# A graph layer pair on one core: the node's own term written into PSUM by ScalarE for two of four graphs, and the extra edges' rows made by products and a comparison

## Chip, core and metric

The kernel runs on one core of a Trainium2 chip. TensorE (PE) multiplies matrices into PSUM, VectorE (DVE), ScalarE (ACT) and GpSimd (POOL) compute element by element, and SyncE (SP) issues most transfers. Each engine works through its own queue in order and waits on semaphores for the others. The metric is device time in microseconds of one execution; the kernel before took 977.03 us, the median of three runs (973.62 to 977.51).

## What is computed

There are 128 graphs of 128 nodes with 64 features. Layer 0 sums, over the edges of each node, a small network of both ends; layer 1 multiplies with the weighted adjacency and a weight matrix.

```python
# layer 0, h = relu(layernorm(x)), mask = adj > 0
W1a, W1b = W1[:F], W1[F:]
diff = h[:, :, None, :] - h[:, None, :, :]
e = relu((h @ W1a)[:, :, None, :] + diff @ W1b + b1)     # (128, 128, 128, 192)
hm = einsum('bjkh,bjk->bjh', e, mask)
x = x + hm @ W2 + deg[..., None] * b2
# layer 1
h = relu(layernorm(x))
x = x + einsum('bnf,of->bno', einsum('bnm,bmf->bnf', adj, h), W)
```

The hidden layer splits into a part that depends on the node j alone (its own term) and a part that depends on the neighbour k alone. So an edge costs one addition of two rows, a relu and a sum. About 12% of the entries of adj are edges.

## The kernel before

Graphs are taken four at a time (G = 4, 32 groups). Within a graph the 128 neighbours are cut in four quarters, and each node gets six slots per quarter (D = 6). One-hot columns S3 say which neighbour sits in which slot; a product with k3 (three bf16 parts of the projected rows, stacked on 96 partitions) then fetches the neighbour's row. Edges beyond six in a quarter go another way, the extra edges: up to 128 per graph are listed, their rows fetched by S2 (neighbour) and R (node), rectified into X and given back to the nodes by RT.

The main work of a group is 24 jobs (class Job, L815), here called places t = 0 to 23 in the list ORDER (L916). A job takes a g tile, two PSUM banks of 128x512 f32. Of kind 0 are the first 128 hidden units of one graph b, a half jh of the nodes and a pair qp of quarters; of kind 1 are the other 64 units of two graphs at once. Six jobs make one run of the order: four of kind 0 (graph r, then graph r + 2, both qp), two of kind 1; it goes r = 0 with both halves, then r = 1 with both. So graphs 0 and 2 have t = 0 to 3 and 6 to 9, graphs 1 and 3 have t = 12 to 15 and 18 to 21, and kind 1 has t = 4, 5, 10, 11, 16, 17, 22, 23.

- Job.fill (L830), TensorE: for kind 0 two fetch products of 384 columns (g<-S,k) start the two banks, and four own-term products of 192 columns (g<-id,k) add the node's own row to all six slots. Kind 1 has twice as many, half as wide in units.
- Job.drain (L851): kind 0 is one VectorE reduction of absolute values (hm<-g); kind 1 is one ScalarE relu into T (T<-g), and GpSimd adds T up.

There are three g tiles (pool ps_g, bufs=3), which the projection tiles pp of pre_proj share, and two single-bank m tiles (ps_m) for all other products. Tables hang the rest of the work between the jobs: AHEAD (L890) prepares the next group, OWN (L905) fetches the extra edges' rows of this one, BEHIND (L909) finishes the one before. At t = 0 stands pre_adj (pt, adjT, maskT), at 1 edge_sum of the last group (pe0) and pre_rank (pq, qs), at 2 pre_norm and pre_hT (ph), at 4 edge_sum1, at 5 pre_count (pd), at 7 pre_proj for two graphs (pp; ScalarE takes ca, z and e from it, VectorE rest, GpSimd the third part of ca), at 8 post0 (py, ys), at 9 pre_edge_a (pv), at 10 post1 (pty, x1 and its statistics), at 12 pre_proj for the other two, at 14 and 15 edge_x (px, X), at 16 post3 (pga), at 19 post4 (po, the result), at 19 to 23 pre_edge_b, pre_place (pj, qj), pre_edge_c (prt, RT) and pre_edge_d (pgq, S2).

R(j, e) is 1 where extra edge e belongs to node j. It is made in steps: pre_edge_a (L620) counts by a product with a triangle how many extra edges lie before each node, and takes four absolute distances to the node's middle on ScalarE (et<-iov,mid); pre_edge_b (L649) applies four relus with the node's half width (et<-et,half) and one more for all (R<-et,ones).

All TensorE work keeps the order of the program text; on the other engines a scheduler decides the order when the kernel is built. The last group has a mixed order (ORDERL), the first runs with an order of its own (ORDER0).

Of the kernel before, what the change touches and what calls it, by code (L numbers as in the profile page):

```python
# [8 lines left out]
F32 = mybir.dt.float32  # L9
BF16 = mybir.dt.bfloat16  # L10
# [140 lines left out]
def kernel(  # L151
# [28 lines left out]
    def mm(*args, **kw):  # L180
        return tc.keep_in_program_order(nc.tensor.matmul(*args, **kw))  # L181
# [46 lines left out]
    with ExitStack() as main:  # L228
# [8 lines left out]
        def gtile(name):  # L237
            return ps_g.tile([P, 2, 512], F32, tag="g", name=name)

        def mtile(name):  # L240
            return ps_m.tile([P, 512], F32, tag="m", name=name)
# [49 lines left out]
        id32 = const.tile([P, QN], F32, tag="id32", name="id32")  # L291
        id3 = const.tile([P, QN], BF16, tag="id3", name="id3")
        upb = const.tile([P, P], BF16, tag="upb", name="upb")
        ioe = const.tile([P, E], F32, tag="ioe", name="ioe")

        def constants():
            vec.tensor_copy(identb, ident)
            vec.tensor_reduce(
                id32, ident.rearrange("p (q j) -> p j q", q=Q), AX.X, ALU.add
            )  # L300
            vec.tensor_copy(id3, id32)
            vec.tensor_copy(upb, upper)
            vec.tensor_scalar(ioe, iov, BIG, None, ALU.add)
    

# [67 lines left out]
        def weights_d():  # L373
            pl = mtile("pl")
            tp(pl[:, 0:P], wl1, ident)
            vec.tensor_copy(wl1t, pl[:, 0:P])
# [132 lines left out]
        def pre_count(g):  # L509
            d = groups[g]  # L510

            pd = mtile(f"pd{g}")
            for b in range(G):
                mm(
                    pd[:, b : b + 1], d["maskT"][:, b, :], negb, start=True, stop=True
                )
                mm(
                    pd[:, G + b : G + b + 1], d["ov"][:, b, :], oneb[:, 0:1], start=True, stop=True
                )
            d["dn"] = grp.tile([P, 2, G], F32, tag="dn", name=f"dn{g}")  # L520
            vec.tensor_copy(d["dn"].rearrange("j t b -> j (t b)"), pd[:, 0 : 2 * G])

            d["ns"] = grp.tile([P, G], F32, tag="ns", name=f"ns{g}")
            vec.scalar_tensor_tensor(
                d["ns"], pd[:, G : 2 * G], float(Q * D), d["dn"][:, 0], ALU.add, ALU.subtract
            )

            d["half"] = tmp.tile([P, G], F32, tag="half", name=f"half{g}")
            vec.tensor_scalar(
                d["half"], pd[:, G : 2 * G], -0.5, 0.5, ALU.mult, ALU.add  # L530
            )
            d["nb"] = tmp.tile([P, G], BF16, tag="nb", name=f"nb{g}")
            vec.tensor_copy(d["nb"], pd[:, G : 2 * G])

        def pre_proj(g, r):
# [67 lines left out]
            if r == 1:  # L603
                add_x()

        def pre_stack(g):

            d = groups[g]
            d["k3"] = grp.tile([K3, Q, 2, G, H], BF16, tag="k3", name=f"k3{g}")
            order = [(part, q) for part in range(3) for q in range(Q)]  # L610
            if g == 0:
                order = [(part, q) for qp in range(2) for part in range(3) for q in (2 * qp, 2 * qp + 1)]
            for part, q in order:
                sp.dma_start(
                    d["k3"][part * QN : (part + 1) * QN, q],
                    d["ca"][q * QN : (q + 1) * QN, part],
                )


        def pre_edge_a(g):  # L620
            d = groups[g]
            pv = mtile(f"pv{g}")
            mm(pv[:, 0:G], upb, d["nb"], start=True, stop=True)
            mm(pv[:, G : 2 * G], oneb, d["nb"], start=True, stop=True)
            vec.tensor_tensor(ovf, ovf, pv[:, G : 2 * G], ALU.max)

            mid = tmp.tile([P, G], F32, tag="mid", name=f"mid{g}")
            vec.tensor_tensor(mid, d["half"], pv[:, 0:G], ALU.subtract)
            d["et"] = tmp.tile([P, G, E], F32, tag="et", name=f"et{g}", bufs=1)
            for b in range(G):  # L630
                act.activation(d["et"][:, b, :], iov, AF.Abs, bias=mid[:, b : b + 1])

        def pre_place(g):

# [10 lines left out]
            )  # L645
            d["qj"] = tmp.tile([P, G, N], BF16, tag="qj", name=f"qj{g}", bufs=1)
            act.activation(d["qj"].rearrange("j b k -> j (b k)"), pj, AF.Copy)

        def pre_edge_b(g):  # L649

            d = groups[g]
            for b in range(G):
                act.activation(
                    d["et"][:, b, :], d["et"][:, b, :], AF.Relu, bias=d["half"][:, b : b + 1]
                )
            d["R"] = grp.tile([P, G, E], BF16, tag="R", name=f"R{g}")
            act.activation(d["R"], d["et"], AF.Relu, bias=ones[:, 0:1], scale=-1.0)

        def pre_edge_c(g):
            d = groups[g]  # L660
# [21 lines left out]
        def edge_x(g, r):  # L682
            d = groups[g]
            if r == 0:
                d["X"] = grp.tile([P, G, H], F32, tag="X", name=f"X{g}", bufs=1)
            px = mtile(f"px{g}_{r}")
            for p in range(2):
                b = 2 * p + r
                for t, one_hot in enumerate(("S2", "R")):
                    for i in range(3):  # L690
                        mm(
                            px[:, p * H : (p + 1) * H], d[one_hot][:, b, :], d["ca"][:, i, t, b],
                            start=t + i == 0, stop=t + i == 3,
                        )
            pxv = px[:, 0 : 2 * H].rearrange("e (p u) -> e p u", p=2)
            act.activation(d["X"][:, r::2, 0:C0], pxv[:, :, 0:C0], AF.Abs)
            act.activation(d["X"][:, r::2, C0:H], pxv[:, :, C0:H], AF.Relu)
# [114 lines left out]
            sp.dma_start(out[g * G : (g + 1) * G].rearrange("b n o -> n b o"), ot)  # L812


        class Job:  # L815
            def __init__(self, g, kind, b, jh, qp):
                self.g, self.kind, self.b, self.jh, self.qp = g, kind, b, jh, qp
                self.gt = gtile(f"g{g}_{kind}_{b}_{jh}_{qp}")

                if kind == 0:  # L820
                    self.parts = [(b, slice(0, C0), slice(0, P))]
                else:
                    self.parts = [
                        (2 * p + b, slice(C0, H), slice(p * C1, (p + 1) * C1)) for p in range(2)
                    ]

            def cols(self, rows, i):
                return self.gt[rows, i, 0:ND].rearrange("h (d j) -> h d j", d=D)

            def fill(self):  # L830

                d = groups[self.g]
                j0 = self.jh * JH
                for i in range(2):
                    q = 2 * self.qp + i
                    for b, us, rows in self.parts:
                        mm(
                            self.cols(rows, i), d["k3"][:, q, 0, b, us],
                            d["S3"][:, q, :, b * N + j0 : b * N + j0 + JH],
                            start=True, stop=False, skip_group_check=True,  # L840
                        )
                for w in range(2):
                    for i in range(2):
                        for b, us, rows in self.parts:
                            mm(
                                self.cols(rows, i)[:, :, w * QN : (w + 1) * QN],
                                d["k3"][:, 2 * self.jh + w, 1, b, us], bc(id3[0:K3, :], D, 1),
                                start=False, stop=w == 1, skip_group_check=True,
                            )
# [43 lines left out]
            7: (lambda g: pre_proj(g, 0),),  # L893
            9: (pre_edge_a,),
            12: (lambda g: pre_proj(g, 1), pre_stack,),
            19: (pre_edge_b,),
            20: (pre_place,),
            21: (pre_edge_c,),
            23: (pre_edge_d,),
        }  # L900
        OWN = {
            14: (lambda g: edge_x(g, 0),),
# [64 lines left out]
        for zs, es, second, third, add_x in steps:  # L967
# [6 lines left out]
        first_slots(0, 3)  # L974
        Engine.held = False
        early = {(f, 1) for f in (pre_adj, pre_norm)}
        FIRST = {
            2: pre_edge_a, 4: pre_place, 6: lambda g: weights_d(), 7: pre_edge_b, 9: pre_edge_d, 10: pre_edge_c
        }
        for g in range(NG):  # L980
            if 0 < g < NG - 1:
                load(g + 1)
            order = ORDER0 if g == 0 else ORDERL if g == NG - 1 else ORDER
            for t, args in enumerate(order):
                job = Job(g, *args)
                job.fill()
                job.drain()
                if g == 0 and t in FIRST:
                    FIRST[t](0)
                pieces(OWN, t, g)  # L990
                pieces(BEHIND, t, g - 1)
                pieces(AHEAD, t, g + 1)
        for t in range(T):
            pieces(BEHIND, t, NG - 1)
        om = one.tile([P, 1], F32, tag="om", name="om")
# [34 lines left out]
```

## Time and profile before

| | us |
|---|---|
| median of three runs | 977.03 |
| the profiled execution | 977.56 |
| its span, first to last instruction | 975.9 |
| VectorE drains hm<-g, 512 of 947 ns | 476.7 |
| TensorE fetch products g<-S,k, 2048 | 385.3 |
| TensorE own-term products g<-id,k, 4096 | 381.6 |
| ScalarE drains T<-g, 256 of 820 ns | 209.4 |
| ScalarE et<-iov,mid, 128 of 389 ns | 40.5 |
| ScalarE et<-et,half, 128 of 447 ns | 56.6 |
| ScalarE R<-et,ones, 32 of 759 ns | 24.3 |

The profile is of one execution. Busy times of different engines overlap, so they don't add up to the span. Products are pipelined and the profile models their ends, so a product's length in the table is more than it costs TensorE; that is read from the distances of starts, as the chain of waits lists them. The granted TensorE clock was 0.986 on the mean and full in the steady part.

### The profile page before, as it was taken

The page shows a single profiled execution, that of the slowest core. Times are in us where ns is not written, and L with a number is a line of the kernel's source. Part 1 is how long each engine was busy: PE and PEld are TensorE (multiplying, and loading weights), DVE is VectorE, ACT ScalarE, POOL GpSimd, SP SyncE. Part 2 cuts the span into 40 slices and gives each one's busy share as a digit, 9 for nine tenths or more (in the row PEclk, how much of TensorE's full clock was granted, in tenths as well). Part 3 has the DMA queues.
Part 4 walks back from the last instruction along what each step waited for, and adds up shares of the span by engine and source line. Part 5 has one row for each costly group of instructions (what it writes and reads, how often), then busy time and mean ns, then how long its engine had stood idle before and what let it go on. Part 6 is the DMA issues. An engine that isn't in the chain of part 4 may idle for free.

```text
span 975.9 us, 26737 instructions
## 1 busy us (share of the span) xinstructions
PE 944.8 (97%) x9994; PEld 692.0 (71%) x9994; DVE 798.1 (82%) x1882; ACT 699.7 (72%) x1732; POOL 745.2 (76%) x1128
## 2 busy tenths in 40 slices
PE   3899999999999999999999999999999999999996
PEld 2577777777777777777777777777777767777774
DVE  6688888888888888888888888888888888888863
ACT  5757877667887667787667887667887767787752
POOL 1478877778877778877778877778787778787793
PEclk9799999999999999999999999999999999999997
DMA  3645765655766655676655676655676655666520
GB/s 86 145 103 133 164 152 135 140 127 130 161 155 141 138 125 128 157 158 141 135 128 122 161 158 141 139 130 128 148 160 144 142 120 129 148 153 139 121 47 13
DMA packets 88293, 129.89 MB, mean 133 GB/s; under 512 B 47200, under 2 KB 63968, under 8 KB 88160
## 3 DMA queue, kind: packets, MB, share of 16 engines
q1 hardware_dynamic: 87584, 127.98, 57.9%
q8 instruction: 80, 1.31, 0.6%
q14 instruction: 53, 0.43, 0.2%
q10 hardware_dynamic: 576, 0.16, 0.1%
HBM read 13.01 MB, written 4.19 MB: 18 GB/s over the span
## 4 chain that ended last, share of the span: by engine, by line
PE 85%; DVE 5%; ACT 4%; DMA 2%; POOL 1%; issue 1%; SPq 1%; DVEq 0%; POOLq 0%; ACTq 0%
PE g L181 49%; PE pe L181 9%; PE pp L181 6%; PE px L181 6%; PE py L181 4%; PE pga L181 1%; PE po L181 1%; DVE u L198 1%; DVE S L198 1%; PE pt L184 1%; PE pj L181 1%; PE ph L184 1%; PE pty L184 1%; DVE hm L198 1%; DMA k<-ca 1%; PE pgq L181 1%
## 5 line engine op out<-in xcount | busy, mean ns | idle before, releaser
L198 POOL TENSOR_TENSOR T<-T 128x192 f32<-128x192 f32 (+2 forms) x768 | 526.7, 693 | 96.1 <-ACT T L198 56.2
L198 DVE TENSOR_REDUCE hm<-g 128x64 f32<-128x768 f32 x512 | 476.7, 947 | 85.1 <-PE g L181 83.2
L181 PEld LDWEIGHTS <-k 96*128 96x128 bf16 (+1 forms) x6144 | 412.2, 104 | 185.5 <-issue 60.7
L181 PE MATMUL g<-S,k 96*128 96x384 bf16 (+1 forms) x2048 | 385.3, 331 | 9.2 <-DMA k<-ca 7.7
L181 PE MATMUL g<-id,k 96*128 96x192 bf16 (+1 forms) x4096 | 381.6, 247 | 0.0
L198 ACT ACTIVATE T<-g 128x768 f32<-128x768 f32 x256 | 209.4, 820 | 75.1 <-PE g L181 74.1
L198 POOL TENSOR_TENSOR ca<-rest,ca 128x384 bf16<-128x384 f32 x126 | 112.6, 914 | 106.5 <-ACT ca L198 101.4
L198 ACT ACTIVATE ca<-pp 128x768 bf16<-128x768 f32 x64 | 51.4, 803 | 61.6 <-PE pp L181 59.8
L198 DVE TENSOR_TENSOR rest<-pp,ca 128x768 f32<-128x768 f32 x64 | 60.8, 950 | 16.1 <-ACT e L198 12.7
L198 ACT ACTIVATE ca<-rest 128x768 bf16<-128x768 f32 x64 | 55.1, 862 | 22.8 <-DVE rest L198 22.8
L198 DVE TENSOR_SCALAR S<-qs 128x512 bf16<-128x512 bf16 x186 | 70.5, 431 | 0.0
L181 PE MATMUL pe<-RT,X 128*64 128x128 f32 (+1 forms) x512 | 70.5, 280 | 0.0
L181 PE MATMUL pp<-wp,hT 64*128 64x448 f32 x256 | 67.8, 608 | 0.0
L198 ACT ACTIVATE z<-pp,ns 128x128 f32<-128x128 f32 (+1 forms) x256 | 65.9, 347 | 0.0
L198 ACT ACTIVATE et<-et,half 128x128 f32<-128x128 f32 x128 | 56.6, 447 | 0.0
L181 PEld LDWEIGHTS pe<-RT,X 128*64 128x64 f32 (+1 forms) x512 | 52.6, 165 | 5.3 <-issue 5.3
L198 ACT ACTIVATE qs<-pq 128x512 bf16<-128x512 f32 x32 | 19.1, 596 | 51.7 <-PE pq L181 51.7
L181 PE MATMUL px<-ca,S 128*128 128x192 bf16 x384 | 52.7, 246 | 0.0
L181 PE MATMUL px<-ca,R 128*128 128x192 bf16 x384 | 52.6, 246 | 0.0
L198 ACT ACTIVATE h<-x,mrb,rsb 128x64 f32<-128x64 f32 x128 | 51.5, 477 | 0.8 <-DVE mrb L198 0.8
L181 PE MATMUL pe<-ident,z 128*128 128x128 f32 x192 | 49.5, 285 | 0.0
L198 ACT ACTIVATE h<-x,mra,rsa 128x64 f32<-128x64 f32 x128 | 48.6, 432 | 1.1 <-DVE mra L198 1.1
(127 smaller groups left out, 1203.9 us busy)
## 6 DMA issues: line engine op xcount, KB each, us to landing
S<-S SPq DMA_DIRECT2D x372, 192.0 KB, 4.1
k<-ca SPq DMA_DIRECT2D x384, 96.0 KB, 2.2
adj<-in_adj_dram SPq DMA_DIRECT2D x32, 256.0 KB, 2.9
x<-in_x_dram SPq DMA_DIRECT2D x32, 128.0 KB, 2.7
out_dram<-ot SPq DMA_DIRECT2D x32, 128.0 KB, 2.2
w<-in_L_gnn_W_dram SPq DMA_DIRECT2D x2, 96.0 KB, 4.3
bias<-in_L_gnn_b_dram ACTq DMA_DIRECT2D x1, 96.0 KB, 3.8
w2a<-in_L_gnn_W_dram ACTq DMA_DIRECT2D x1, 32.0 KB, 2.2
```

The source lines that it names most:

```text
L181: return tc.keep_in_program_order(nc.tensor.matmul(*args, **kw))
L184: return tc.keep_in_program_order(nc.tensor.transpose(*args, **kw))
L198: ins = f(*args, **kw)
```

## The change

Three things are changed.

1. For graphs 0 and 2 of every group but the first, the own-term products are left out of the kind-0 jobs. pre_own makes the own term of these graphs as a matrix of units by nodes in SBUF, `at` (six products with the identity, one VectorE copy), at t = 17 of the group before. Job.seed has ScalarE copy it, repeated over two banks and six slots, into the g tile; the two fetch products then add to what is there. The loop takes the g tile of the next job, and issues its seed, after the pieces of the present place.
2. R is now a product and a comparison: two 512-column products put, for every graph and extra edge, the number of extra edges before the node less e and a half into PSUM, and VectorE compares this, read as integers, with the negated count. The nine ScalarE operations of pre_edge_a and pre_edge_b are gone.
3. The product and the maximum that watch for too many extra edges (ovf) move from pre_edge_a into edge_x at t = 14.

```diff
+            vec.tensor_scalar(ioh, iov, -1.0, -0.5, ALU.mult, ALU.add)
...
-                d["half"], pd[:, G : 2 * G], -0.5, 0.5, ALU.mult, ALU.add
+                d["half"], pd[:, G : 2 * G], -1.0, None, ALU.mult
...
+        def pre_own(g):
+            d = groups[g]
+            pa = mtile(f"pa{g}")
+            for p in range(2):
+                for i in range(3):
+                    mm(
+                        pa[:, p * N : (p + 1) * N], d["ca"][:, i, 1, 2 * p, 0:C0], identb,
+                        start=i == 0, stop=i == 2,
+                    )
+            d["at"] = grp.tile([P, 2, N], F32, tag="at", name=f"at{g}")
+            vec.tensor_copy(d["at"].rearrange("u p n -> u (p n)"), pa[:, 0 : 2 * N])
...
         def pre_edge_a(g):
             d = groups[g]
             pv = mtile(f"pv{g}")
-            mm(pv[:, 0:G], upb, d["nb"], start=True, stop=True)
-            mm(pv[:, G : 2 * G], oneb, d["nb"], start=True, stop=True)
-            vec.tensor_tensor(ovf, ovf, pv[:, G : 2 * G], ALU.max)
-
-            mid = tmp.tile([P, G], F32, tag="mid", name=f"mid{g}")
-            vec.tensor_tensor(mid, d["half"], pv[:, 0:G], ALU.subtract)
-            d["et"] = tmp.tile([P, G, E], F32, tag="et", name=f"et{g}", bufs=1)
-            for b in range(G):
-                act.activation(d["et"][:, b, :], iov, AF.Abs, bias=mid[:, b : b + 1])
+            pvb = pv.rearrange("j (b e) -> j b e", b=G)
+            mm(pvb, upb, bc(d["nb"], E, 2), start=True, stop=False)
+            mm(pvb, oneb[0:1, :], bc(ioh[0:1, :], G, 1), start=False, stop=True)
+            d["R"] = grp.tile([P, G, E], BF16, tag="R", name=f"R{g}")
+            vec.tensor_tensor(
+                d["R"], pvb.bitcast(I32), bc(d["half"].bitcast(I32), E, 2), ALU.is_lt
+            )
...
-        def pre_edge_b(g):
-
-            d = groups[g]
-            for b in range(G):
-                act.activation(
-                    d["et"][:, b, :], d["et"][:, b, :], AF.Relu, bias=d["half"][:, b : b + 1]
-                )
-            d["R"] = grp.tile([P, G, E], BF16, tag="R", name=f"R{g}")
-            act.activation(d["R"], d["et"], AF.Relu, bias=ones[:, 0:1], scale=-1.0)
...
+            if r == 0:
+                mm(px[:, 2 * H : 2 * H + G], oneb, d["nb"], start=True, stop=True)
+                vec.tensor_tensor(ovf, ovf, px[:, 2 * H : 2 * H + G], ALU.max)
...
+        SEEDED = (0, 2)
+
         class Job:
...
+                self.seeded = g > 0 and kind == 0 and b in SEEDED
...
+            def seed(self):
+                j0 = self.jh * JH
+                own = groups[self.g]["at"][:, self.b // 2, j0 : j0 + JH]
+                act.activation(
+                    self.gt[:, :, 0:ND].rearrange("h i (d j) -> h i d j", d=D),
+                    bc(bc(own, D, 1), 2, 1), AF.Copy,
+                )
...
-                            start=True, stop=False, skip_group_check=True,
+                            start=not self.seeded, stop=self.seeded, skip_group_check=True,
                         )
+                if self.seeded:
+                    return
...
-            19: (pre_edge_b,),
...
+            17: (pre_own,),
...
-                job = Job(g, *args)
+                job = ahead or Job(g, *args)
                 job.fill()
                 job.drain()
+                ahead = None
...
+                ng, na = (g, order[t + 1]) if t + 1 < T else (g + 1, orders(g + 1)[0])
+                if ng < NG:
+                    ahead = Job(ng, *na)
+                    if ahead.seeded:
+                        ahead.seed()
```

More of the change, by code (lines that the diff above doesn't have):

```diff
@@ L293 @@
         upb = const.tile([P, P], BF16, tag="upb", name="upb")
+        ioh = const.tile([P, E], BF16, tag="ioh", name="ioh")
         ioe = const.tile([P, E], F32, tag="ioe", name="ioe")
@@ L976, with orders @@
         early = {(f, 1) for f in (pre_adj, pre_norm)}
+        def orders(g):
+            return ORDER0 if g == 0 else ORDERL if g == NG - 1 else ORDER
+        ahead = None
         FIRST = {
-            2: pre_edge_a, 4: pre_place, 6: lambda g: weights_d(), 7: pre_edge_b, 9: pre_edge_d, 10: pre_edge_c
+            2: pre_edge_a, 4: pre_place, 6: lambda g: weights_d(), 9: pre_edge_d, 10: pre_edge_c
         }
@@ L982 @@
                 load(g + 1)
-            order = ORDER0 if g == 0 else ORDERL if g == NG - 1 else ORDER
+            order = orders(g)
             for t, args in enumerate(order):
-                job = Job(g, *args)
+                job = ahead or Job(g, *args)
                 job.fill()
                 job.drain()
+                ahead = None
                 if g == 0 and t in FIRST:
```

## The prediction

> **What bounds the kernel now.** I read the page's busy times first, then the chain that ended last, then one group of four graphs in order of time, then busy times of its two stretches.
>
> ```profile
> PE 944.8 (97%) x9994; PEld 692.0 (71%) x9994; DVE 798.1 (82%) x1882; ACT 699.7 (72%) x1732; POOL 745.2 (76%) x1128
> ...
> PE 85%; DVE 5%; ACT 4%; DMA 2%; POOL 1%; issue 1%; SPq 1%; DVEq 0%; POOLq 0%; ACTq 0%
> ```
>
> TensorE is busy nearly always, and 85% of the span's chain runs over it. In the chain, one group (places t=22 of the last to t=12 of the next) reads:
>
> ```profile
> 464.76 1.43 PE g L181 x24
> 466.19 0.33 PE pgq L181 x4
> 466.52 0.66 PE g L181 x6
> 467.18 0.44 PE pt L184 x4
> 467.61 0.13 issue
> 467.74 0.95 PE g L181 x6
> 468.69 2.02 PE pe L181 x24
> ...
> 476.67 1.06 PE pp L181 x6
> ```
>
> Each row is a start, a length and the products issued in it. A kind-0 fill is "g x6" in 0.66 us; a kind-1 fill is twelve products in about 0.72. One group takes 29.14 us (from the "pga" of one group at 489.06 to that of the next at 518.20). Two stretches of it, by engine:
>
> ```profile
> core 0: us, PE busy (x) PEld busy (x) DVE busy (x) ACT busy (x) POOL busy (x), PEclk, DMA share, GB/s
> 466.50:482.20 15.70, 15.57 (x162) 10.88 (x159) 13.78 (x27) 8.73 (x20) 10.70 (x17) 1.00 0.45 98
> 482.20:495.65 13.45, 13.45 (x153) 10.24 (x150) 10.89 (x31) 12.66 (x35) 12.32 (x19) 1.00 0.76 177
> ```
>
> The first stretch is t=0 to 11, the second t=12 to 23. All eight fills that the change lightens lie in the first, where VectorE is already at 13.78 of 15.70.
>
> **What the change takes from TensorE and adds.** In "px", twelve products of 192 columns take 0.99 us, 0.0825 each, and the four 192-column own-term products are half of a fill: 4 x 0.0825 = 0.33. Eight fills a group: -2.64 us. Added: six 128-column products in pre_own, at 0.056 each (the four of "prt" take 0.22 to 0.23): +0.34; two 512-column products in pre_edge_a at 0.21 ("pq", one such, 0.21): +0.42, less 0.02 for the tiny ones that go. Net -1.90 us in each of 31 groups; group 0 is not seeded and pays 0.40. If nothing else happened, that would be -58 us.
>
> **ScalarE.** Gone per group: four Abs of 389 ns, four Relu of 447, one of 759 (the "et" and "R" rows): -4.1 us, all from the second stretch. Added: eight seeds of 128x768. No row shows ScalarE writing PSUM. Nearest below: "qj<-pj", 128x512 out of PSUM, 597 ns, a shorter tile, so a floor. Nearest above: "ca<-rest", 128x768 from SBUF, 862. "T<-g", 128x768 f32 with PSUM at the other end, is 820, and is nearest in size and type: I take 0.82, and 0.70 until the next may start (a T at 465.64 is followed at 466.34). Eight are +6.6 us, in the first stretch: 8.7 becomes 15.3.
>
> The Trainium skill (ScalarE: Activation LUTs, "Step-by-step: what each stage is for") says that ScalarE writes PSUM faster than SBUF, and its page Perfetto Trace Analysis ("Optimizing Scalar/DVE Operations") puts the difference of the two memories at about 40 ns an access. By that rule a seed would be an estimated 0.78 and the loss below some 6 us less; no row of this trace has such a write.
>
> **VectorE.** Added: the comparison into R, 128x512 out of PSUM, like "S<-pgq" at 691 ns; the copy of the own term, 128x256 out of PSUM, like "x<-pty" at 417. Gone: "mid", 150. Net +0.96 us a group, 24.6 to 25.6: below the period, so no bound by itself.
>
> **The wait that is added.** A fill with products that add onto a seed cannot start before the seed has ended, and a seed needs its g tile drained. Only three g tiles exist, shared with "pp". Before, TensorE filled up to three tiles ahead of the drains; now drain, seed and fill form a loop, and a seed stands in ScalarE's one queue behind evacuations that wait for TensorE itself. I follow the order of the changed program's instructions with durations of this trace; hand-over between engines costs 0.04 us (pq ends 499.96, qs starts 500.00). Zero is the start of t=22's fill.
>
> ```profile
> 495.09 0.81 ACT L198 ACTIVATE T<-g 128x768 f32<-128x768 f32 x1 [0.24 <-PE g L181]
> ...
> 500.00 0.60 ACT L198 ACTIVATE qs<-pq 128x512 bf16<-128x512 f32 x1 [1.60 <-PE pq L181]
> ```
>
> In these rows of ScalarE's time line, the first is the drain of a t=22, which waited for its fill; the bracket tells the idle time before a row and who ended it.
>
> At t=0 and 1 ScalarE's queue is drain of t=22, seed 0, drain of t=23, seed 1. The t=22 drain starts at 0.95 (as 495.09 against 494.14), seed 0 at 1.65, and ends at 2.47. TensorE is done with "pgq" at 1.76 and waits 0.75. It fills (0.33) and transposes (0.44) until 3.28; seed 1 started at 3.05 and ends at 3.88: wait 0.63. So "pe" starts at 4.24 where before it did at 3.93 (468.69): two fills were lightened by 0.66 and 1.38 was waited.
>
> At t=2 and 3 seeds 2 and 3 hide under the 2.02 us of "pe". "ph" waits for the drain of "pe" by VectorE until 7.32, 0.5 us, as its cover, the fill of t=2, is now 0.33 shorter (0.2 to 0.3 more than before); t=3 keeps its 0.33.
>
> From "ph" on TensorE has 0.44, t=3 0.33, t=4 0.72, "pe1" 0.95, t=5 0.69 and "pd" 0.28: it reaches t=6 at 10.73. Seed 6 stands behind the drain of t=4 (9.07 to 9.88) and ends at 10.74; seed 7, 0.70 behind it, at 11.44: wait 0.38. "pp" needs the tile of t=5, whose drain stands behind seed 7: 12.13, wait 0.36. Seed 8 needs VectorE's drain of t=6 (behind its work on S, u and "pd" until 11.62, so 12.57) and ends at 13.43: wait 0.24. Seed 9 needs the drain of t=7 (13.66) and ends at 14.52; only then come the evacuations of "pp", 2.15 us (477.77 to 479.92), and "ys": "pty" waits 0.42. The waits come to 0.75 + 0.63 + 0.5 + 0.38 + 0.36 + 0.24 + 0.42 = 3.3, of which some 0.7 was there before (the issue row, "ph", uneven fills). So the second "pp" starts at 18.7 where before it was 18.3 (483.07 less 464.76): 2.64 saved, 0.42 added, 2.6 waited anew.
>
> From t=12 on: VectorE starts "rest" when the evacuation of "pp" ends, 1.4 us later than before, and behind it stand R (0.69), x, the statistics and the drain of t=12: VectorE is about 1 us late, and TensorE, with full fills again, has no room to catch up. On VectorE: rest until 17.56, R 18.16, x 18.48, statistics 19.36, drains of t=12, 13 and 14 with more statistics (0.95) between them until 23.0, the second rest 23.9. On ScalarE behind it: ca 24.8 and, after that in its queue now, X 25.3, which before stood ahead of ca. "pga" needs X's bank. TensorE itself, 5.95 us from "pp" to "pga" (483.07 to 489.06), is there at 24.6: wait 0.74. Then pre_own, +0.34. ScalarE's removed Relus hide nothing here: it was not on the chain.
>
> Sum from t=22 to "pga": 25.34, against 24.0 to 24.3 before, then +0.34: 1.4 to 1.7 a group, 1.5 taken. 31 x 1.5 = +46 us on the profiled 975.9 span; the same on the median of 977.03 (the profiled run was 977.56): 1022 us. A POOL or SP queue is not moved past; the last third of ca, which POOL writes and SP sends on into k3, is done some 4 us before t=22 against 3 before (491.2 and 494.2), so these transfers are not the last to come.
>
> A rule of the skill speaks against gain from another side: Perfetto Trace Analysis, "Identifying the Most-Contended Engine", takes weight-load time, not matmul time, as TensorE's headroom. The row has 71%: by that rule TensorE had room, taking products away would gain nothing, and the 58 us would fall out of the sum, leaving only losses; by the row of the second stretch, matmuls in 13.45 of 13.45 us with weight loads in 10.24, they are there to be had. I keep them.
>
> **Rivals.** (a) Seeds are hidden: all wait is gone, and the 58 us are gained: 977 - 58 = 919. For it: 97% and 85% above, and ScalarE's idle rows, 1.6 to 2.0 us before "qs". Against: a seed is issued one place ahead, never two, and the order puts seeds 0 and 1 behind drains that start only when TensorE gets there. 5%.
> (b) Short seeds, the side that ends not slower. Place: the five spots where a seed's length is on TensorE's path (once at t=0, once at t=1, twice before "pp", once before "pty"). At the floor, 0.60, each saves 0.22, 1.1 a group, and VectorE's lateness goes with it and the 0.74 at "pga": 1.5 - 1.84 = -0.34 a group, 966 us. It decides below about 0.66 us a seed, where 5 x 0.16 + 0.7 makes up the 1.5. For it: the source in SBUF is a small tile. Against: "ca<-rest" with its source in SBUF is the slower of the rows. 17%, of which 6% stay within 0.5%.
> (c) Same loop, but the wait at "pga" does not come, because VectorE is less late: 1.5 - 0.74 = 0.8 a group, 1002 us. For it: a lateness of 1 us is a difference of long sums. 15%.
> (d) Seeds of 1.1 us, as two banks and a repeated source might cost more than any row: five times 0.28 more, 2.9 a group, 1067. No row speaks for it. 5%.
>
> **Numbers.** The forecast itself, 1010 to 1035, has 58%; what a measurement here can tell from no change is 0.5%, about 5 us. Slower: 58 + 15 + 5 = 78%. Same: 6%. Faster: 5 + 11 = 16%. The range runs from 960, which takes in most of (b), to 1045, which takes seeds at 0.89, the longest T row. Outside lie (a), (d) and the ends, under 20%. The likeliest case's own range is 1010 to 1035.
>
> **What would show it.** Right: "PE g" waits for an ACT writing g, some 0.7 us at t=0 and 0.6 at t=1 in each group; PE busy near 87% (887 of 1020 us); "pga" waits for X; a seed row of 0.75 to 0.9 us; a period of 30.4 to 30.8. Wrong: a seed under 0.66, or a t=12 to 23 stretch of 13.8 us without waits. I would be wrong most simply if VectorE's drains of t=6 and 7 come earlier than I have them, since seeds 8 and 9 and all behind them hang on those.

## The result and the profile after

The changed kernel takes 1038.51 us (median of four runs, 1032.86 to 1039.27) against 977.27 for the kernel before (973.62 to 981.05): a ratio of 1.0621, 95% interval 1.0586 to 1.0655. It is 61 us slower; 46 were forecast. The time lies within the stated range of 960 to 1045, 3.5 us above the likeliest case's 1010 to 1035. Runs of one kernel differ by some 5 us with the granted clock (here 1032.86 at a mean of 0.993, the other three 1037.87 to 1039.27 at 0.984 to 0.986), so small differences between kernels are compared below at like clock. The profiled execution took 1037.87 us with a span of 1036.1.

The busy times of the changed kernel:

```profile
PE 915.0 (88%) x9220; PEld 626.6 (60%) x9220; DVE 827.8 (80%) x1914; ACT 802.7 (77%) x1692; POOL 746.0 (72%) x1128
```

TensorE falls from 97% busy to 88% while the span grows by 60 us, so it now waits. The same two stretches of one group as before the change, t=0 to 11 and t=12 to 23:

```profile
core 0: us, PE busy (x) PEld busy (x) DVE busy (x) ACT busy (x) POOL busy (x), PEclk, DMA share, GB/s
495.30:511.40 16.10, 13.89 (x130) 8.46 (x128) 13.25 (x25) 13.18 (x24) 9.41 (x16) 1.00 0.45 96
511.40:526.43 15.03, 14.19 (x162) 10.83 (x159) 12.23 (x34) 11.96 (x31) 13.87 (x21) 1.00 0.76 177
```

The first stretch, where all the lightened fills lie, has 1.7 us less TensorE work than before (13.89 for 15.57) and is still 0.4 longer (16.10 for 15.70). The second, where no fill changed, went from 13.45 to 15.03, with 0.84 of idle TensorE that was not there. ScalarE's first stretch rose from 8.73 to 13.18, less than the 15.3 forecast: a seed starts 0.1 before the operation ahead of it ends, and the busy time counts overlaps once; besides, three "h" operations (1.09 us together) stood in this stretch before and stand ahead of it now.

The waits of the changed kernel: who waited for whom, us in all, times, the longest:

```profile
PE g L181 <- ACT g L198: 44.7, 91, 1.0
...
ACT g L198 <- DVE hm L198: 21.5, 60, 1.0
...
PEld ph L184 <- DVE u L198: 21.0, 30, 0.8
PEld pga L181 <- ACT X L198: 20.0, 30, 0.7
PEld pp L181 <- ACT T L198: 18.9, 30, 0.6
...
PE pga L181 <- ACT X L198: 13.5, 30, 0.5
...
PE g L181 <- DVE hm L198: 10.4, 27, 0.4
```

Some 90 times a fill waits for a seed, three times a group; "ph", "pga", "pp" and one more fill wait once a group each. The time line of TensorE shows where (start, length, and in brackets the idle time before the row and who ended it). These rows are one group; its t=22 fill starts at 493.47.

```profile
496.01 0.48 PE L181 MATMUL g<-S,k 96*128 96x384 bf16 x2 [0.71 <-ACT g L198]
...
497.44 0.48 PE L181 MATMUL g<-S,k 96*128 96x384 bf16 x2 [0.51 <-ACT g L198]
...
504.89 0.48 PE L181 MATMUL g<-S,k 96*128 96x384 bf16 x2 [0.25 <-ACT g L198]
505.62 1.02 PE L181 MATMUL pp<-wp,hT 64*128 64x448 f32 x4 [0.24 <-ACT T L198]
...
516.11 0.48 PE L181 MATMUL g<-S,k 96*128 96x384 bf16 x2 [0.38 <-DVE hm L198]
...
519.16 0.66 PE L181 MATMUL pga<-adjT,h 128*64 128x128 f32 x8 [0.46 <-ACT X L198]
```

From above: t=0, t=1 and t=7 wait for a seed, the first "pp" for the drain of t=5, t=15 for a VectorE drain, "pga" for X. ScalarE's time line at t=0 and 1 is the queue that the prediction wrote down, drain, seed, drain, seed:

```profile
494.44 0.81 ACT L198 ACTIVATE T<-g 128x768 f32<-128x768 f32 x1 [0.27 <-PE g L181]
495.15 0.81 ACT L198 ACTIVATE g<-at 128x768 f32<-128x768 f32 x1
495.88 0.81 ACT L198 ACTIVATE T<-g 128x768 f32<-128x768 f32 x1
```

The seed and the drain last the same, 0.81, and each starts 0.70 to 0.73 after the one ahead. The fill of t=0 cannot start before 495.15 + 0.81, and TensorE is at it 0.7 earlier.

To say where a group's time goes, the time lines of TensorE were cut at four starts, "pgq" (t=23), "ph" (t=2), the second "pp" (t=12) and "pga" (t=16), and the median taken over 27 groups. The forecast column is the prediction's own times: "pgq" starts 0.33 before the 1.76 at which it ends, "ph" is 7.32, the second "pp" 18.7, "pga" 25.34, and pre_own adds 0.34 to the 6.68 that lay behind "pga". The kernels are told in the experiments.

| us per group | pgq to ph | ph to pp | pp to pga | pga to pgq | period |
|---|---|---|---|---|---|
| before | 5.13 | 11.44 | 5.89 | 6.68 | 29.14 |
| forecast | 5.89 | 11.38 | 6.64 | 7.02 | 30.93 |
| changed kernel | 5.89 | 11.38 | 6.98 | 6.88 | 31.13 |
| e1, rows alone | 5.02 | 11.94 | 6.38 | 6.59 | 29.93 |
| e6, rows alone, ovf moved | 5.02 | 11.94 | 5.80 | 6.59 | 29.35 |
| e5, changed, ovf moved | 5.89 | 11.38 | 6.35 | 6.86 | 30.48 |
| e2, seeds alone | 7.12 | 11.38 | 5.84 | 6.88 | 31.22 |
| e8, t=0 and 1 not seeded | 5.02 | 11.39 | 6.98 | 6.88 | 30.27 |
| e11, no seed, ovf moved | 4.85 | 10.98 | 5.80 | 6.85 | 28.36 |
| e10, two seeds | 5.10 | 11.46 | 5.84 | 6.59 | 28.91 |

The two stretches where the seeds stand came out as forecast. The change costs 1.99 a group, 62 us in 31 groups, and that is the 61 measured.

### The profile page after: what moved, and what is told of

Its sections match the earlier page's. It is cut to its first block, busy times and chain, and to the rows that moved or that the text cites. A ratio compares the mean times of both kernels' runs of the same rounds, so it can differ in the third digit from the quotient of the medians.

```text
span 1036.1 us, 25431 instructions
## 1 busy us (share of the span) xinstructions
PE 915.0 (88%) x9220; PEld 626.6 (60%) x9220; DVE 827.8 (80%) x1914; ACT 802.7 (77%) x1692; POOL 746.0 (72%) x1128
## 5 line engine op out<-in xcount | busy, mean ns | idle before, releaser
L181 PEld LDWEIGHTS <-k 96*64 96x64 bf16 (+1 forms) x5152 | 329.9, 105 | 234.9 <-issue 141.0
L181 PE MATMUL g<-S,k 96*128 96x384 bf16 (+1 forms) x2048 | 381.0, 331 | 69.0 <-ACT g L198 44.7
L181 PE MATMUL g<-id,k 96*64 96x192 bf16 (+1 forms) x3104 | 260.3, 247 | 0.0
L198 ACT ACTIVATE g<-at 128x768 f32<-128x768 f32 x248 | 197.0, 813 | 22.4 <-DVE hm L198 21.5
L198 DVE TENSOR_SCALAR S<-qs 128x512 bf16<-128x512 bf16 x186 | 67.3, 416 | 0.0
L198 DVE RECIPROCAL rsa<-sda 128x4 f32<-128x4 f32 x32 | 5.7, 177 | 56.3 <-ACT sda L198 56.3
L198 ACT ACTIVATE h<-x,mra,rsa 128x64 f32<-128x64 f32 x128 | 45.9, 429 | 5.9 <-DVE mra L198 2.3
L198 POOL TENSOR_TENSOR hm<-T 128x64 f32<-128x64 f32 x128 | 41.3, 323 | 10.0
```

The source lines that it names most:

```text
L198: ins = f(*args, **kw)
```

## The experiments

Every kernel was timed against the kernel before on the same chip (medians of the kernel before: 975.79 for e1 to e4, 977.28 for e5 to e8, 976.47 for e9 to e11). Ratios stand with their 95% interval.

### e1: parts 2 and 3 of the change alone

```diff
-        SEEDED = (0, 2)
+        SEEDED = ()
...
-            17: (pre_own,),
```

> The rows R by products and a comparison alone, no graph seeded, no pre_own. Theory (the loss is the seeds' wait): TensorE pays 0.40 us more a group, VectorE 0.54, and ScalarE is freed of 4.1 us that were not on the chain: 977 + 13 = 990 us, between 975 and 1000. Rival (the loss comes with the new rows, through VectorE's comparison ahead of the statistics and drains): at least 1015 us.

Measured: 1000.8 us, 1.025 (1.023 to 1.027), just outside what was expected. One wait of e1:

```profile
PE pga L181 <- ACT X L198: 11.7, 29, 0.7
```

Without one seed "pga" waits for X all the same, which the kernel before does nowhere. So this wait is no consequence of the seeds, as the prediction had it. It comes with the new rows or with the moved maximum.

### e2: part 1 alone

pre_edge_a, pre_edge_b, `half` and edge_x are as before the change, pre_own and the seeds as after it.

> The seeds alone, R made by ScalarE as before. Theory: the waits at t=0 to 9 stay (seed 0.7 us and seed 1 0.5 us on TensorE), and ScalarE's nine operations come back into a second stretch that is already late: 1040 to 1075 us. Rival (the new rows are the loss): below 1000 us.

Measured: 1043.83 us, 1.0693 (1.0654 to 1.0731), as expected. The seeds alone lose the whole of it, and a little more. In this kernel the wait at "pga" is absent (pp to pga 5.84) and the stretch to "ph" is 1.2 longer than in the changed kernel; there "pq" waits 0.64 for maskT and "ph" 0.76 for u, so ScalarE's and VectorE's other work sits behind the seeds in place of it. Neither wait is in the lists of e5 or of the changed kernel at such a size (there "ph" waits 0.31), so once there are seeds, the new rows take something off.

### e3: the seeds not written

The first fetch product starts the bank; nothing is written by Job.seed. This leaves out the own term of graphs 0 and 2.

```diff
-                            start=not self.seeded, stop=self.seeded, skip_group_check=True,
+                            start=True, stop=self.seeded, skip_group_check=True,
...
-                    if ahead.seeded:
-                        ahead.seed()
```

> The changed kernel with no seed written: the fetch products of graphs 0 and 2 start their banks, so the own term of these graphs is left out of the result. Theory: with the seeds' wait gone the lightened fills are worth their TensorE time, 27.3 us a group: 915 to 950 us. Rival (lightened fills are worth little, because VectorE's drains bound the first stretch anyway): 970 us or more.

Measured: 960.64 us, 0.9853 (0.9832 to 0.9873), outside both ranges. Writing the seeds and waiting for them costs 78 us (1038.5 less 960.6), but the lighter fills are worth less than the sum of the removed products: the wait at "pga" is there too, and in some groups the fill of t=8 waits 0.63 for a VectorE drain.

### e4: seeds half as long

One bank is seeded, the other is started by its fetch product; this leaves out the own term in the second bank.

```diff
-                    self.gt[:, :, 0:ND].rearrange("h i (d j) -> h i d j", d=D),
-                    bc(bc(own, D, 1), 2, 1), AF.Copy,
+                    self.gt[:, 0, 0:ND].rearrange("h (d j) -> h d j", d=D),
+                    bc(own, D, 1), AF.Copy,
...
-                            start=not self.seeded, stop=self.seeded, skip_group_check=True,
+                            start=not self.seeded or i == 1, stop=self.seeded, skip_group_check=True,
```

> Each seed writes one of the two banks (128x384 in place of 128x768); the other bank's own term is left out. Theory: a seed of some 0.55 us, 0.26 less at five places of TensorE's path, and part of the 0.7 at pga: 1.3 to 2.0 us a group, 975 to 998 us. Rival (it is the hand-over and the queue order, not the length of a seed): 1020 us or more.

Measured: 1053.16 us, 1.0794 (1.074 to 1.0847), the wrong way. The seeds are shorter, 494 ns on the median. At t=0 and 1 ScalarE's queue is still drain, seed, drain, seed, and TensorE waits 0.32 less at each, which is all of what the seed is shorter (0.71 and 0.51 in the changed kernel):

```profile
473.45 0.48 PE L181 MATMUL g<-S,k 96*128 96x384 bf16 x2 [0.39 <-ACT g L198]
...
474.56 0.48 PE L181 MATMUL g<-S,k 96*128 96x384 bf16 x2 [0.19 <-ACT g L198]
```

Further on the scheduler ordered ScalarE's queue anew. In e4's time line of ScalarE:

```profile
483.66 0.79 ACT L198 ACTIVATE ca<-pp 128x768 bf16<-128x768 f32 x1
...
485.64 0.42 ACT L198 ACTIVATE ys<-py 128x256 f32<-128x256 f32 x1
485.90 0.55 ACT L198 ACTIVATE g<-at 128x384 f32<-128x384 f32 x1
```

The seed of t=9 stands behind the whole evacuation of "pp", 2.2 us, where the changed kernel has it ahead, and the fill of t=9 waits 1.02 for it. Cut as in the table, e4 has 5.37, 12.10, 7.17 and 6.88: the first stretch is 0.52 shorter than the changed kernel's, the second 0.72 longer, the period 0.39 longer (31.52). That is 12 us in 31 groups; the rest of the 15 goes with the clock (in two groups of the profiled run it was 0.85, and these took 34.83). So a shorter seed is worth its whole difference where nothing moves, and one seed's worse place in the queue costs more than that.

### e5 and e6: the maximum taken out of edge_x

After e1 the theory was that part 3 makes the wait at "pga". In e5, the changed kernel, the product and the maximum for ovf go to the tile of pre_own at t=17 (group 0 keeps them in edge_x). e6 is e1 with the same move into a tile of its own, so it has neither seeds nor a maximum on px.

```diff
+            mm(pa[:, 2 * N : 2 * N + G], oneb, d["nb"], start=True, stop=True)
...
+            vec.tensor_tensor(ovf, ovf, pa[:, 2 * N : 2 * N + G], ALU.max)
...
-            if r == 0:
+            if r == 0 and g == 0:
```

> The changed kernel with the product and the maximum of ovf taken out of the px tile and put into the tile of pre_own, so that ScalarE's X no longer waits for VectorE there. Theory: the wait at pga (0.65 us a group) is made by that maximum, which stands behind the late second rest on VectorE, and goes: 1038 - 20 = 1018 us, between 1010 and 1025. Rival (the wait is VectorE's general lateness, as the prediction had it): 1030 us or more.

> The new rows alone, as in the run without seeds, with ovf in a tile of its own that only VectorE reads. Theory: 1001 less the wait at pga, 0.6 us a group: 978 to 988 us, TensorE's added products (13 us) and nothing else. Rival (the comparison on VectorE costs by itself): 995 us or more.

Measured: e5 1020.1 us, 1.0439 (1.0421 to 1.0456), 18 less than the changed kernel; e6 983.73 us, 1.0052 (1.0026 to 1.0078), 17 less than e1. Both as expected. The cause is seen by laying two time lines side by side. First VectorE and then ScalarE of the changed kernel, ahead of the "pga" at 519.16:

```profile
516.84 0.94 DVE L198 TENSOR_TENSOR rest<-pp,ca 128x768 f32<-128x768 f32 x1
517.71 0.14 DVE L198 TENSOR_TENSOR ovf<-ovf,px 128x4 f32<-128x4 f32 x1
```

```profile
517.82 0.84 ACT L198 ACTIVATE ca<-rest 128x768 bf16<-128x768 f32 x1 [1.01 <-DVE rest L198]
518.57 0.97 ACT L198 ACTIVATE X<-px 128x256 f32<-128x256 f32 x4
```

The maximum, 0.14 us long, is placed behind "rest", and all of X stands on ScalarE behind the copy of "rest", after 1.01 us in which ScalarE had nothing to do. The products of the first px had ended at some 515.7. In e5:

```profile
502.01 0.59 ACT L198 ACTIVATE X<-px 128x256 f32<-128x256 f32 x2
...
503.84 0.84 ACT L198 ACTIVATE ca<-rest 128x768 bf16<-128x768 f32 x1 [0.58 <-DVE rest L198]
504.59 0.53 ACT L198 ACTIVATE X<-px 128x256 f32<-128x256 f32 x2
```

Half of X is ahead of "ca" again, its bank is free, and "pga" starts without a wait:

```profile
504.54 0.60 PE L181 MATMUL pga<-adjT,h 128*64 128x128 f32 x8
```

Whether X waits for the maximum itself or only for its new place in the order was not separated. What e5 does not remove is the wait of t=15 for a drain (0.40 there, 0.38 in the changed kernel); neither e6 (no seeds, pp to pga 5.80) nor e2 (seeds with the old rows, 5.84) shows such a wait, so it takes both, the seeds and the new rows' comparison on VectorE.

### e7: seeded and plain jobs in turn

If the loop of drain, seed and fill is the trouble, a plain job between two seeded ones should give the seed time. Graphs 0 and 1 are seeded instead of 0 and 2, and their jobs alternate with those of graphs 2 and 3.

```diff
...
-        SEEDED = (0, 2)
+        SEEDED = (0, 1)
...
-            17: (pre_own,),
+            22: (pre_own,),
...
-                ORDER += [(0, b, jh, qp) for b in (r, 2 + r) for qp in range(2)]
+                ORDER += [(0, b, jh, qp) for qp in range(2) for b in (2 + r, r)]
```

> Seeded and unseeded jobs by turns: graphs 0 and 1 are seeded, each run of four kind-0 jobs is unseeded, seeded, unseeded, seeded; ovf as in the run that moves it. The same eight seeds. Theory: no two seeds follow each other on ScalarE, a full fill of 0.66 us stands before each, and t=0 needs none, so most of the waits at t=0 to 9 go: 960 to 1000 us. Rival (any seed one place ahead waits for its drain and for the queue, however spread): 1010 us or more.

Measured: 1067.54 us, 1.091 (1.0884 to 1.0936): the rival holds. Waits of e7:

```profile
ACT g L198 <- DVE hm L198: 97.3, 93, 2.5
PE g L181 <- ACT g L198: 75.4, 66, 1.5
```

Now the seed itself stands at the head of ScalarE's queue for up to 2.5 us, waiting until VectorE has drained its tile, and everything on ScalarE waits with it. A plain job between two seeds does not help. That it takes one of the three g tiles as well is a likely reason, but it was not tested apart: in e7 half of the seeds also moved into the second stretch, and pre_own to t=22.

### e8: t=0 and 1 filled in full

```diff
-                self.seeded = g > 0 and kind == 0 and b in SEEDED
+                self.seeded = g > 0 and kind == 0 and b in SEEDED and (b, jh) != (0, 0)
```

> The changed kernel with graph 0's first two jobs, t=0 and 1, not seeded; six seeds a group in place of eight. Theory: 0.7 and 0.5 us of wait go, 0.66 of own-term products come back: 0.55 us a group, 1038 - 17 = 1021 us, between 1013 and 1028. Rival (the wait only moves on to the next place): 1034 us or more.

Measured: 1008.51 us, 1.0307 (1.0275 to 1.034), better than expected. In the table pgq to ph goes from 5.89 to 5.02 and nothing else moves: two full fills are 0.87 a group cheaper than two seeded ones. In e8 fills wait for seeds 10.5 us in all, against 44.7 in the changed kernel:

```profile
PE g L181 <- ACT g L198: 10.5, 35, 1.0
```

### e9: seeds two places ahead

e5 with the g tile of a seeded job taken, and its seed issued, two places ahead rather than one.

```diff
-                    ahead = Job(ng, *na)
-                    if ahead.seeded:
-                        ahead.seed()
+                for k in (1, 2):
...
+                    pending.append(Job(ng, *na))
+                    if pending[-1].seeded:
+                        pending[-1].seed()
```

> As the run that only moves ovf, and the g tile of a seeded job is taken, and its seed issued, two places ahead in place of one (not in the last group). Theory: seed 0 now runs before the drain of t=22 and the wait at t=0 goes, about 0.55 us for t=0 and 1 together, and the seeds of t=6 and 7 come half a place earlier: 0.5 to 1.2 us a group off 1020, 983 to 1005 us. Rival (the seeds are bound by the tiles' drains, not by their place in the queue): 1013 us or more.

Measured: 1026.11 us, 1.0514 (1.0481 to 1.0546), slower than e5 (1020.1). The time misleads here. In the 23 of 29 middle groups of the profiled run that had the full clock the median period is 30.35 against e5's 30.48, 0.13 shorter; the other 6 groups, at a granted clock of 0.95, took 31.9. All four runs of e9 have a low mean clock (0.973 to 0.976, e5 0.983 to 0.989), and why is open. Without these groups the profiled run would have taken an estimated 1017 us (1026.9 less 6 x 1.57). So two places ahead gain a little at best, far from the 0.5 to 1.2 us a group that the theory had. The largest new wait in e9's time line:

```profile
528.97 1.02 PE L181 MATMUL pp<-wp,hT 64*128 64x448 f32 x4 [1.24 <-DVE hm L198]
```

A seed that is earlier takes its tile earlier. With three tiles shared with "pp", much of the time that the fills gain is lost again where "pp" finds no tile free: the stretches of the table are 5.62, 11.80, 5.80 and 7.13, so "ph" comes 0.27 earlier than in e5, the second "pp" 0.42 later after it, and "pga" 0.55 sooner after that.

### e10: only the two seeds that have cover

Rows and ovf are as before the change; only t=2 and 3 (graph 2, first half of the nodes) are seeded, in the shadow of the 2 us of "pe", and pre_own makes that half alone, with three 64-column products.

```diff
-                self.seeded = g > 0 and kind == 0 and b in SEEDED
+                self.seeded = g > 0 and kind == 0 and (b, jh) == (2, 0)
```

> Two seeds a group only, those of t=2 and 3 (graph 2, first half of its nodes), whose ScalarE time lies under the 2.0 us of pe; R and ovf as in the kernel before; the own term is made for 64 nodes of one graph. Theory: 0.66 us of products less, 0.3 lost again at ph, some 0.15 for pre_own: 0.1 to 0.5 us a group faster than before, 961 to 974 us. Rival (any seed costs more than the products it replaces): 980 us or more.

Measured: 971.11 us (eight runs), 0.9951 (0.9928 to 0.9973): some 5 us faster than the kernel before, the fastest complete kernel of this study, though not by much (29.03 a group against 29.20 on the mean of the middle groups, 5 us in all). In its time line of ScalarE both seeds end before their fills (468.35 and 469.03) are due:

```profile
465.96 0.80 ACT L198 ACTIVATE g<-at 128x768 f32<-128x768 f32 x1
466.70 0.58 ACT L198 ACTIVATE adjT<-pt 128x512 f32<-128x512 f32 x1
467.17 0.81 ACT L198 ACTIVATE g<-at 128x768 f32<-128x768 f32 x1
```

Of the 0.66 a group that the fills lose, less 0.1 for pre_own, 0.23 reaches the median period. In most groups the fill of t=8 now waits 0.3 for a VectorE drain (6.9 us in all in 23 waits; in the kernel before 0.9 in 3), which takes back what t=3 gained. And adjT stands behind a seed, maskT behind adjT, and "pq" waits for it:

```profile
468.13 0.38 PE L181 MATMUL pq<-maskT,triq 128*128 128x512 bf16 x1 [0.23 <-DVE maskT L198]
```

### e11: no seed written, ovf moved

e3 with e5's move; the own term of graphs 0 and 2 is left out.

> No seed is written, as in the run without seeds (the own term of graphs 0 and 2 is left out of the result), and ovf as in the run that moves it. Theory: 961 less the wait at pga, 0.6 us a group: 935 to 947 us; the distance to the run that only moves ovf, 1020, is then what the eight seeds cost by waiting. Rival (VectorE is the bound once fills are light): 953 us or more.

Measured: 948.88 us, 0.9719 (0.9689 to 0.975), just above the range. Against e5 (1020.1), which differs by the eight seeds alone, the seeds cost 71 us by the medians, 68 at like clock (1020 at 0.984, 952.3 at 0.985). Against e6 (983.73), which has full fills and no pre_own, the lighter fills are worth 35 us by the medians and some 31 at like clock (983 to 985 at 0.985 against 952.3; 978.5 at 0.992 against 947.2 to 949.3 at 0.991), and 32 by the mean periods (29.35 and 28.33 in 31 groups). So the change spends about 70 to gain 30 to 35.

## Why the forecast came out as it did

**The sum.** Taken in turn: the new rows with ovf apart +6 us (977 to 984, e6), the lighter fills -35 (949, e11), the seeds and the waits for them +71 (1020, e5), the maximum in edge_x +18 (1038.5). That is the mechanism forecast, lost saving and new waits, and one part that was put down to the wrong cause. The parts do not simply add, though, and the split depends on the order: with the seeds first (e2, 1043.8), the new rows with ovf apart (e5, 1020.1) give 24 us back.

The period should grow by 1.5 and grew by 1.99. The 0.49 is made up of 0.29 from the base of the sum and 0.34 from "pp" to "pga", less 0.14 for pre_own; each has its paragraph below.

**TensorE's own work.** Net -1.90 a group was forecast. A lightened fill is 0.32 to 0.33 long (496.01 to the next start at 496.33), as forecast. By the two stretches one group has 28.08 us of busy TensorE where it had 29.02, 0.94 less and not 1.90; the end of a product is modelled, and one that is followed by a wait counts in full, so this is a bound from below. By that count TensorE's idle time a group went from 0.13 to 3.05, and 2.92 more idle less 0.94 of work is the 1.98 of the period. e11 shows what of the saving can be had, 31 to 35 us, and it is far from nothing. The Trainium skill (Perfetto Trace Analysis, "Identifying the Most-Contended Engine") has the share of weight loads, beside the share of peak arithmetic (MFU), as a measure of the distance to the roofline, in place of the share of matmuls. That at 71% of weight loads taking products away would gain nothing was the prediction's own conclusion from it, and e11 against e6 shows that it does not hold here. The gain is also far from the whole: in e11's middle groups TensorE is busy some 27.2 of 28.3 us, "ph" waits for VectorE's u (21 us in all for its weights), and fills for VectorE drains (12.4, up to 0.7) and for the transfers of k (16.2, of which 6.8 once).

**The seed.** 0.82 taken, 0.813 measured, next start 0.73 later against 0.70. The rule of a cheaper write to PSUM (ScalarE: Activation LUTs, "Step-by-step: what each stage is for") gave 0.78, because the 40 ns were taken off "T<-g", which has PSUM at one end already: the copy from SBUF into PSUM and the rectified copy from PSUM into SBUF last 813 and 814 ns. The row of this size with SBUF at both ends, "ca<-rest", lasts 839 ns in the changed kernel, so a write to PSUM is the faster one here too, by 26 ns (its output is bf16, so the two are not alike in all). Rival (b) needed 0.66 and falls, as does (d) with 1.1.

**t=0 to the second "pp".** Waits of 0.75 and 0.63 at t=0 and 1: measured 0.71 and 0.51. t=7: 0.38, measured 0.25. "pp": 0.36, measured 0.24. These brackets count from the modelled end of the product before; by starts t=0 comes 0.86 later after "pgq" than before the change, and t=1 0.67 later after "pt". "ph" at 7.32: 7.33. Second "pp" at 18.7: 18.71, with some luck behind "py": the wait of 0.42 at "pty" came to 0.14 by starts, and from the two products of "pv" to the next fill it is 0.63, where 0.42 was booked. Writing the changed queue out instruction by instruction was worth its length.

**t=0 and 1 by themselves.** The prediction held 1.38 of waiting against 0.66 saved, and took "pe" to be 0.31 later than before, at 4.24 against 3.93. e8 says 0.87, and that is 0.86 and 0.67 by starts less the 0.66. The 4.24 was good (497.77 less 493.47 is 4.30). The 3.93 was not the usual time of the kernel before, which takes 1.43 to "pgq" and 1.99 from there, 3.42 in all.

**The base of the sum.** This is one of the two terms that were mis-sized. "25.34, against 24.0 to 24.3 before" subtracted from the new time that of one group, the one whose fill of t=22 starts at 464.76 in the chain, and this group is not a usual one. In the time line of the kernel before, the prediction's group first, then the next:

```profile
466.12 0.40 PE L181 MATMUL pgq<-R,qj 128*128 128x128 bf16 x4
...
468.53 0.27 PE L181 MATMUL pe<-ident,z 128*128 128x128 f32 x1
...
495.57 0.40 PE L181 MATMUL pgq<-R,qj 128*128 128x128 bf16 x4
...
497.56 0.28 PE L181 MATMUL pe<-ident,z 128*128 128x128 f32 x1
```

From "pgq" to "pe" it is 2.41 in the prediction's group and 1.99 in the next, as on the median. From "pga" to "pga" the prediction's group took 29.45; the 29.14 that it names is the next one's. (Starts read from the chain and from the time line differ too, but only by some 0.1 here: 24.30 and 24.20 from t=22 to "pga".) By medians the kernel before takes 5.13 + 11.44 + 5.89 from "pgq" to "pga" and 1.43 ahead of that, 23.9. The prediction's own places give 30.93 a group, +1.79 or 55 us; it wrote 1.5 and 46, and its sign, a period of 30.4 to 30.8, was too low with it (31.13).

**From "pp" to "pga".** Forecast 6.64, measured 6.98. The prediction has one wait here, 0.74 at "pga", from VectorE being 1 us late because of the seeds, with X behind "ca" in ScalarE's queue. The place and the order were right and the size nearly so (a bracket of 0.46, and 0.63 from e5's 6.35 to 6.98), but the cause was wrong, so the size was luck: e1 has the wait without seeds, e5 loses it with all seeds. It was part 3, a tiny reader added to px, for which the prediction has no term. Rival (c), no wait at "pga", 1002 us, is the state of e5: 1020, since the base was 0.29 short and t=15 still waits 0.40 for the late VectorE. That wait is what the lateness really costs, and the forecast had none at t=15.

**pga to pgq.** pre_own +0.34 forecast, +0.20 measured: before the change "po" was followed by a gap of 0.13, which went.

**The new rows.** +0.40 a group was booked for their products; e6 has +0.50 from "ph" to "pp" and -0.29 elsewhere, 6 us in all. The comparison took 680 ns (691 forecast) and the copy 410 (417). The relief of ScalarE was put at nothing on the chain. Without seeds it gives at most the 0.29. With seeds it gives more: "pgq" to "ph" takes 7.12 with the old rows (e2) and 5.89 with the new (e5).

**What stays open.** How the time depends on the length of a seed beyond t=0 and 1 (e4 changed the order there), why e9 ran at a lower clock, and whether X waits for the maximum or only for its place.

## What to carry to other kernels

An operand preset by another engine turns a fill that could run ahead into a loop of drain, seed and fill: count the tiles, find the one who drains them, and write the seeding engine's queue out in order before counting the saved products. Here it paid only where the seed lay under other work that was already there, at t=2 and 3, and little even there. Price the small movements of a diff too: a reader of four columns, put on a tile that another engine evacuates, cost 18 us here. And before one group's time is taken as the base of a sum, compare it with the median of many: here the group taken was 0.3 us longer than most, which is 9 us in 31 groups. Look at the granted clock in the same way before a small difference is explained.

## What was not expected of the hardware and the scheduler

- ScalarE writes 128x768 f32 into PSUM from a repeated source of 64 columns in 813 ns, the same as it takes out of PSUM into SBUF (814), and 26 less than "ca<-rest" with SBUF at both ends (839); half the size takes 494.
- A kernel edited at one tile has its queues on ScalarE and VectorE ordered anew in places that the edit does not touch: e4's shorter seeds ran 12 us slower than the full ones at like clock (1049 to 1051 at 0.983 to 0.984, 1037.9 to 1039.3 at 0.984 to 0.986), and a 0.14 us maximum moved X behind a 0.84 us copy.
- In the changed kernel no engine is over 88% busy and no wait of TensorE in a group is over 0.71 us; the seven of the time line (0.71, 0.51, 0.31 at "ph", 0.25, 0.24, 0.38, 0.46) add to 2.86 us, nearly all of its 3.05 of idle time.
